# Two wide multiplications of the fp4 rounding move to GpSimd for three late chunks

## The chip, the cores and the metric

The kernel runs on one core of one Trainium2 chip. TensorE multiplies matrices, VectorE (DVE in the profile) and GpSimd (POOL) do elementwise work and reductions, ScalarE (ACT) does activations and copies, and SyncE (SP) issues the DMAs. The metric is the device time of one execution in microseconds (us), as the median of several runs.

## What is computed

The input is x, 8 sequences of 1024 rows of 256 floats. Four stages follow, each as x = x + stage(layernorm(x)): a decoder layer with linear attention and a gelu feed-forward, a relu feed-forward of width 1024, softmax attention over each sequence, and a gated feed-forward whose operands are rounded to fp4. The change touches this last stage:

```python
def fp4_quant_dequant(x):                 # blocks of 16 along the last dimension
    scale = max(abs(xb)) / 6.0            # one per block, at least 1e-12
    q = GRID[searchsorted(MID, abs(xb / scale))] * sign(xb) * scale
gate = fp4_linear(x, w_gate)
y = fp4_linear(x, w_up)                   # 256 -> 704
h = silu(gate) * y
return fp4_linear(h, w_down)              # rounds h (rows of 704) again, 704 -> 256
```

## The kernel before

The rows are cut into 64 chunks of 128 rows, eight to a sequence. The linear attention works on 16 groups of four chunks (`flow` p = 0 to 15), the two dense stages on the same groups, and softmax with the gated stage on single chunks, cc = 0 to 63 (`soft_chunk`, line 1729). All stages run beside each other for different rows. Once the last group has left the linear attention (`linear_attention`, line 1544), its buffers `q` and `k` become two more buffers for gated rows (line 1554); that is why the same operation appears in the profile on `hid`, `q` and `k`, and why `flow`, `x` and `rows` serve beside `prob` and `rows`. Buffer names in the profile are of the tag and not of the stage.

One softmax chunk takes its scores, exponentials, turned probabilities and the product with the values; then a layer norm, the rounding of its 256-wide rows (`fp4(n, D)`, line 1813), the products with the gate and up weights in two halves of 352 columns, tanh on ScalarE and two multiplications on VectorE for each half, and the rounding of the 704-wide gated rows (`fp4(hid, INTER, factor=0.5)`, line 1844). The rounded rows are turned in three pairs of 128 columns (`flip`, line 739), either on TensorE, with a copy by ScalarE, or by a `cut` copy on GpSimd, a transposing DMA to `spun` and a copy by ScalarE. Twelve matmuls with `wdT` (six steps of contraction, each shown as two) give the chunk's output, VectorE adds the rows (`y`), and a DMA stores it.

The rounding (`fp4`, line 802) is, for a width of 704: a reduction to 44 maxima (`x_amax`), the scale `x_s`, its reciprocal `x_r`, a multiplication of the row by `x_r`, a square on ScalarE (`q_c`, kept as bf16), two operations that add and subtract a constant and so round (`hid<-q_c,hid`, twice), and a multiplication by `x_s`. All but the square ran on VectorE.

The order of the instructions is written out by a planner (`Plan`, line 133) while the kernel is built. Each part of the work is a generator that names the queue and the tiles that it needs next; `took` (line 226) estimates what each instruction costs and when its engine and its result are free; `run` (line 380) issues, again and again, the part with the smallest key. The key holds first the wait, then how far the part is from "ripe" (its data must have been there for `ripe_t`, `ripe_v`, `ripe_s`, `ripe_g` or `ripe_d` us, by queue, line 124), then a due time. `idle` (line 365) says whether TensorE has a part ready within `ahead` us; where not, `flip` turns on TensorE. These constants are replaced by others as the planner's clock goes on (`EARLY`, line 78; the last set, line 104, holds from 2150 us of its own clock). `due` (line 470) adds constants that hold for one flow alone (`lin1`, `lin3`). The queue order of each engine is exactly the planner's. Where TensorE would have nothing for 1.6 us, `fill` (line 1883) puts in products of the identity with itself.

Of the kernel before, what the change touches and what calls it, by code (L numbers as in the profile page):

```python
# [14 lines left out]
ALU = mybir.AluOpType  # L15
AX = mybir.AxisListType

P = 128
# [5 lines left out]
INTER = 704  # L24
# [7 lines left out]
    span=-0.073, prods=0.129, pair=0.137, sums=0.037, weighted=0.239, sums2=0.231, chunk=0.625,  # L32
    scores=0.819, turn_k=0.829, xo=0.419, turn_h=0.635, step=0.092, dense=-0.115, norm=0.522,
    soft=3.5, soft1=0.277, soft2=0.575, soft3=0.75, fp4=2.397, fp4_over=4.836, tail=11,
    weights=0.209, shy=0.745, ripe_t=1.247, ripe_v=0.744, ripe_s=0.298, ripe_g=0.0, ripe_d=6.94,
    back=0.511, ahead=0.946, stage=3, lin=0.0, lin0=0.01, lin1=0.0, lin2=0.0, lin3=0.0,
    dense0=0.0, dense1=-0.033, norm0=0.0, norm1=0.0, weights0=-0.412, weights1=0.023, gate0=0,
    gate1=1, gate2=1, by_act=1,
)
LAG = 2  # L40
QB = 16
G = 4
GT = G * P
# [38 lines left out]
        weights=0.082, shy=0.832, ripe_t=0.516, ripe_v=0.135, ripe_s=0.467, ripe_g=0.906,  # L82
        ripe_d=13.418, lin0=-0.645, dense1=-0.003, norm1=-0.276, weights0=-1.017, weights1=0.043,
# [3 lines left out]
        span=-0.064, pair=0.148, sums=-0.114, chunk=0.644, scores=0.581, turn_k=0.911, xo=0.57,  # L87
        dense=0.196, soft=3.213, soft1=0.005, soft2=0.747, fp4_over=6.403, shy=-0.178,
        ripe_t=1.2, ripe_s=0.838, ripe_g=0.043, back=0.505, ahead=0.602, lin=-0.262, lin1=-0.582,
# [6 lines left out]
        weights=0.078, ripe_d=7.107, ahead=0.839, lin2=-0.414, dense1=-0.101, norm1=0.415,  # L96
    )),
    (2150.0, dict(
        span=-0.075, prods=0.106, pair=0.211, sums=0.071, weighted=0.176, chunk=0.596,
# [2 lines left out]
        dense1=0.151, norm0=-0.113, norm1=-0.184, weights0=-0.286, gate1=3, shy=0.438,  # L102
    )),
    (1000000000.0, dict(
        lin3=0.54, ripe_d=5.647, lin1=0.423, dense1=-0.149, scores=0.713, ripe_g=0.203, xo=0.287,
        chunk=0.609, shy=-0.351, back=0.633, sums2=0.302, ripe_t=0.458, soft2=0.808, ahead=1.77,
        step=0.117, span=-0.165, weights=0.128, ripe_s=0.0, fp4=2.485, turn_k=0.743,
    )),
]

# [18 lines left out]
class Plan:  # L129
# [96 lines left out]
    def took(self, queue, op, args, kw):  # L226

        aps = [x for x in list(args) + list(kw.values()) if isinstance(x, bass.AP)]
        outs = [kw["out"] if "out" in kw else aps[0]]
        if kw.get("accum_out") is not None:  # L230
            outs.append(kw["accum_out"])
        size = 1
        for ap in aps:
            n = 1
            for d in ap.shape[1:]:
                n *= d
            size = max(size, n)

        overlap, after = 0.0, 0.035
        if queue == "tensor":  # L240
            size = 1
            for d in outs[0].shape[1:]:
                size *= d
            cost = size * (0.853e-3 if op == "transpose" else 1.687e-3)
            tiled = op == "matmul" and (kw["lhsT"].shape[-1] <= 32 or kw["lhsT"].shape[0] <= 32)
            if tiled or op == "matmul" and kw["lhsT"].dtype == BF16:
                cost *= 0.25
            if tiled != self.tiled:
                cost += 0.2
            self.tiled = tiled  # L250
            after = 0.2
        elif queue == "vector":
            each = {"reciprocal": 6.2e-3, "tensor_tensor_scan": 2.15e-3}.get(op, 1.05e-3)
            cost = 0.17 + each * size
            if op == "tensor_scalar" and outs[0].dtype == BF16:
                cost = 0.16 + 0.26e-3 * size
            elif op == "scalar_tensor_tensor" and any(ap.shape[-1] == 1 for ap in aps):
                cost += 0.06
            if size >= 256 and not any(ap.tensor.name in self.banks for ap in aps):
                cost *= 1.12  # L260
            overlap = 0.08
        elif queue == "scalar":
            cost = (0.16 if op == "copy" and outs[0].dtype != U16 else 0.26) + 0.82e-3 * size
            for x in args:
                if not isinstance(x, bass.AP) and self.SETS.get(x, self.act_set) != self.act_set:
                    self.act_set = self.SETS[x]
                    self.free[queue] = self.free.get(queue, 0.0) + 1.3
            if kw.get("accum_out") is not None:
                cost += 0.15
            overlap = 0.1  # L270
        elif queue == "gpsimd":
            cost = 0.65 + 0.7e-3 * size
            if op in ("tensor_scalar", "iota"):
                cost = 0.22
            elif op == "memset":
                cost = 0.1 + 0.9e-3 * size
            elif op == "tensor_copy":
                cost = 0.2 + 1.0e-3 * size
        else:
            wide = op != "dma_start_transpose" and size > 256  # L280
            cost = 1.34 if op == "dma_start_transpose" else 0.6 if wide else 0.54
        start = self.free.get(queue, 0.0)
        if queue not in ("tensor", "sync"):
            start = max([start] + [self.used.get(ap.tensor.name, 0.0) for ap in outs])
        for ap in aps:
            name = ap.tensor.name
            if self.by.get(name) != queue or queue in ("vector", "gpsimd"):
                start = max(start, self.done.get(name, 0.0) + (0.05 if queue == "gpsimd" else 0.0))
            if name not in self.done and name in self.held:
                start = max(start, self.used[name])  # L290
        if queue == "tensor":
            if start - self.ran > 2.0:
                self.slow = start + 2.1
            if start < self.slow:
                cost *= 2
            self.ran = start + cost
        if queue == "sync":
            start = max(start, self.landed.pop(0))
        end = start + cost
        if queue == "sync":  # L300
            n = 2e-6 / 180e-3 if op == "dma_start_transpose" else 4e-6 / 320e-3
            for d in outs[0].shape:
                n *= d
            self.free["rings"] = max(self.free.get("rings", 0.0), end) + n
            after = self.free["rings"] - end + (0.75 if op == "dma_start_transpose" else 1.8)
            self.landed.append(end + after)
        self.free[queue] = end - overlap
        for ap in outs:
            self.done[ap.tensor.name] = end + after
            self.by[ap.tensor.name] = queue  # L310
        for ap in aps:
            name = ap.tensor.name
            self.used[name] = max(self.used.get(name, 0.0), end + after)
            if queue != "tensor" and name not in self.kept:
                self.held.discard(name)
# [130 lines left out]
def block_stack_kernel(ctx: ExitStack, tc: tile.TileContext, a: dict, out: bass.AP):  # L446
# [20 lines left out]
    plan = Plan(tc, tc.nc)  # L467
# [328 lines left out]
    def blocks(t, width):  # L796
        return t[:, :width].rearrange("p (b e) -> p b e", e=QB)

    def wide(v, rows, nb):
        return v.unsqueeze(2).to_broadcast([rows, nb, QB])  # L800

    def fp4(src, width, rows=P, factor=1.0):

        nb = width // QB
        src = src[:rows, :width]
        amax = small([P, INTER // QB], "x_amax", 2)[:rows, :nb]
        nc.vector.tensor_reduce(
            amax, blocks(src, width), AX.X, ALU.max, apply_absolute_value=True
        )
        sc = small([P, INTER // QB], "x_s", 4)[:rows, :nb]
        nc.vector.tensor_scalar(sc, amax, factor / 6.0, 1e-12, ALU.mult, ALU.max)
        rc = small([P, INTER // QB], "x_r", 3)[:rows, :nb]
        nc.vector.reciprocal(rc, sc)  # L820
        yield dve(rc)
        nc.vector.scalar_tensor_tensor(
            blocks(src, width),
            blocks(src, width),
            -factor * (1.0 - 2.0**-23),
            wide(rc, rows, nb),
            ALU.mult,
            ALU.mult,
        )
        tile_c = yield from fresh("q_c", act(src))  # L830
        c = tile_c[:rows, :width]
        nc.scalar.activation(c, src, AF.Square, scale=(2.0**22 / 6.0) ** 0.5)
        yield dve(c)
        k = 2.0**22 * 4.0 / 3.0
        nc.vector.scalar_tensor_tensor(src, c, k, src, ALU.add, ALU.add)
        yield dve(src)
        nc.vector.scalar_tensor_tensor(src, c, k, src, ALU.add, ALU.subtract)
        plan.drop(tile_c)
        nc.vector.tensor_tensor(
            blocks(src, width), blocks(src, width), wide(sc, rows, nb), ALU.mult  # L840
        )

# [96 lines left out]
    weights = set()  # L939
# [789 lines left out]
    def soft_chunk(cc):  # L1729
# [86 lines left out]
        hid = None  # L1816
# [24 lines left out]
            nc.vector.tensor_tensor(hid[:, cols], hid[:, cols], ub, ALU.mult)  # L1841
        plan.drop(xqT)
        yield dve(hid)
        yield from fp4(hid, INTER, factor=0.5)
        hqT, pairs = [], []
        for half in range(2):
            tq = yield from fresh("prob", plan.pool(hid, at=at + times["soft3"]), "hqT")
# [91 lines left out]
```

## Time and profile before

| what | us |
|---|---|
| median of 3 runs (lowest, highest) | 2448.72 (2447.79, 2450.22) |
| the profiled execution | 2447.88 |
| its span, first to last instruction | 2445.7 |
| TensorE, VectorE, ScalarE, GpSimd busy | 2421.6, 1893.1, 1415.8, 1260.2 |
| 44 maxima of the last five chunks' gated rows taken at | 2399.88, 2411.86, 2413.34, 2417.38, 2428.20 |
| last output added on VectorE at | 2442.57 |

A line of the instructions in order of time has the start, the time taken, engine, line of the kernel (nearly always 427, the planner's helper), operation, output and inputs by their tags, the shape, and how many of the kind stand together; brackets hold the idle time of the engine just before and what ended it. Engines overlap the end of one instruction with the start of the next, so starts can be closer than the durations.

### The profile page before, as it was taken

To read this page: it belongs to the slowest core of one execution; us is meant where nothing else is said; L and a number is where in the kernel's file an instruction comes from. 1 tells how busy PE (TensorE), PEld (TensorE's weight loads), DVE (VectorE), ACT (ScalarE), POOL (GpSimd) and SP (SyncE) were. 2 spreads that over 40 slices of the span, in tenths; PEclk is the share of its full clock that TensorE was granted. 3 is DMA by queue.
4 is the path that set the end of the run, shared out by engine and by line. 5 is a ranking of instruction groups with operands and counts; after the bars stand their busy time and mean duration, and the time that the engine had idled before them with its cause. 6 is when DMAs were issued, how large, how long until landed. Compare 5 with 4: busy or idle time off the path is not lost.

```text
span 2445.7 us, 47558 instructions
## 1 busy us (share of the span) xinstructions
PE 2421.6 (99%) x16449; PEld 1884.0 (77%) x16449; DVE 1893.1 (77%) x4128; ACT 1415.8 (58%) x2936; POOL 1260.2 (52%) x2251
## 2 busy tenths in 40 slices
PE   8999999999999999999999999999999999999999
PEld 6787887877877777777777777778787777877676
DVE  7887777868778787777868778687786878755877
ACT  5546456565555656566565655746657465565563
POOL 4455364555545646366454645545455564544342
PEclk9999999999999999999999999999999999999999
DMA  4454655555555555456464564555565645545341
GB/s 105 108 168 136 177 135 142 126 125 134 126 134 126 138 137 124 131 134 146 119 143 132 130 142 119 133 122 124 142 131 132 139 122 143 126 127 126 65 97 46
DMA packets 627665, 312.34 MB, mean 128 GB/s; under 512 B 430560, under 2 KB 615904, under 8 KB 627424
## 3 DMA queue, kind: packets, MB, share of 16 engines
q1 hardware_dynamic: 627424, 309.31, 52.2%
q8 instruction: 130, 2.13, 0.4%
q14 instruction: 111, 0.91, 0.1%
HBM read 188.43 MB, written 20.97 MB: 86 GB/s over the span
## 4 chain that ended last, share of the span: by engine, by line
PE 83%; DVE 8%; ACT 3%; POOL 2%; issue 2%; DMA 1%; SPq 0%; DVEq 0%; POOLq 0%; ACTq 0%
PE bank L427 83%; DVE prod L427 2%; DVE hid L427 2%; DMA spun<-cut 1%; ACT L427 1%; POOL cut L427 1%; POOL ln_rstd L427 1%; DVE ln_st L427 1%; DVE x_amax L427 0%; DVE u L427 0%; DVE spread L427 0%; POOL ln_shift L427 0%; POOL ln_ve L427 0%; DVE mx L427 0%; DVE res L427 0%
## 5 line engine op out<-in xcount | busy, mean ns | idle before, releaser
L427 PE MATMUL bank<-half,w_in 128*128 128x256 f32 x2048 | 531.0, 382 | 3.1 <-ACT half L427 2.6
L427 PE MATMUL bank<-w_out,hidden 128*128 128x256 f32 x2048 | 526.1, 383 | 1.4 <-ACT hidden L427 1.4
L427 PEld LDWEIGHTS bank<-w_out,hidden 128*128 128x128 f32 x2048 | 376.4, 190 | 100.3 <-issue 44.5
L427 PEld LDWEIGHTS bank<-half,w_in 128*128 128x128 f32 x2048 | 382.8, 190 | 77.1 <-issue 17.2
L427 POOL TENSOR_SCALAR ln_ve<-ln_mv 128x1 f32<-128x1 f32 x384 | 104.5, 272 | 581.7 <-DVE ln_mv L427 554.2
L427 POOL TENSOR_TENSOR ln_rstd<-ln_ve,neghalf 128x1 f32<-128x1 f32 x384 | 236.5, 616 | 31.9
L427 ACT ACTIVATE hidden<-bank,c_L_ffn_b 128x256 f32<-128x256 f32 x256 | 121.1, 473 | 215.4 <-PE bank L427 214.6
L427 PE MATMUL bank<-n2T,qT 128*128 128x512 f32 x512 | 241.8, 595 | 0.2
L427 PE MATMUL bank<-vt,probT 128*128 128x256 f32 x1024 | 231.5, 379 | 0.0
L427 POOL COPY cut<-n 128x512 uint16<-128x512 uint16 x228 | 162.3, 718 | 120.2 <-DVE n L427 85.4
L427 ACT ACTIVATE hidden<-bank,c_L_attn_b 128x256 f32<-128x256 f32 x256 | 120.2, 470 | 175.7 <-PE bank L427 175.0
L427 PEld LDWEIGHTS bank<-vt,probT 128*128 128x128 f32 x1024 | 194.4, 190 | 31.3 <-issue 3.6
L427 POOL COPY cut<-prob 128x512 uint16<-128x512 uint16 x222 | 163.1, 762 | 83.7 <-ACT prob L427 67.0
L427 ACT ACT_TABLE_LOAD x137 | 175.8, 1283 | 12.3 <-PE bank L427 9.1
L427 POOL COPY cut<-hid 128x512 uint16<-128x512 uint16 x165 | 121.5, 755 | 110.0 <-DVE hid L427 66.3
L427 ACT COPY probT<-spun 128x512 uint16<-128x512 uint16 x250 | 162.6, 672 | 25.7 <-DMA spun<-cut 25.3
L427 PE MATMUL bank<-wdT,hqT 128*128 128x256 f32 x768 | 176.6, 380 | 0.8 <-DVE sc L427 0.4
L427 PE MATMUL bank<-wgT,xqT 128*128 128x352 f32 x512 | 173.3, 461 | 0.4 <-DVE sc L427 0.2
L427 PE MATMUL bank<-wuT,xqT 128*128 128x352 f32 x512 | 172.5, 459 | 0.3 <-DVE sc L427 0.3
L427 PEld LDWEIGHTS bank<-wdT,hqT 128*128 128x128 f32 x768 | 145.1, 190 | 23.9 <-issue 1.4
L427 PEld LDWEIGHTS bank<-n2T,qT 128*128 128x128 f32 x512 | 96.1, 190 | 71.2 <-issue 57.6
L427 DVE TENSOR_TENSOR sc<-bank,tri 128x384 f32<-128x384 f32 x240 | 118.1, 545 | 31.8 <-PE bank L427 31.2
(292 smaller groups left out, 4784.4 us busy)
## 6 DMA issues: line engine op xcount, KB each, us to landing
w_in<-in_L_attn_W_dram SPq DMA_DIRECT2D x128, 256.0 KB
w_out<-in_L_attn_W_dram SPq DMA_DIRECT2D x128, 256.0 KB
w_in<-in_L_ffn_w_dram SPq DMA_DIRECT2D x128, 256.0 KB
w_out<-in_L_ffn_w_dram SPq DMA_DIRECT2D x128, 256.0 KB
spread<-packed SPq DMA_DIRECT2D x90, 256.0 KB
spun<-cut SPq DMA_TRANSPOSE x761
x<-in_L_attn_inputs_dram SPq DMA_DIRECT2D x64, 128.0 KB
xr<-in_L_attn_inputs_dram SPq DMA_DIRECT2D x64, 128.0 KB
```

Source lines behind the costliest of these rows:

```text
L427: ins = method(*args, **kw)
```

## The change

For chunks 59, 60 and 61 the multiplication by the reciprocal and that by the scale run on GpSimd (`pooled`). GpSimd's product has no place for the constant factor, so a small multiplication on VectorE puts it into the 44 reciprocals first. The planner's cost of a GpSimd operation wider than 512 is 1.5 us. The last set of due times is replaced.

```diff
+POOLED = (59, 62)
...
-        lin3=0.54, ripe_d=5.647, lin1=0.423, dense1=-0.149, scores=0.713, ripe_g=0.203, xo=0.287,
-        chunk=0.609, shy=-0.351, back=0.633, sums2=0.302, ripe_t=0.458, soft2=0.808, ahead=1.77,
-        step=0.117, span=-0.165, weights=0.128, ripe_s=0.0, fp4=2.485, turn_k=0.743,
+        lin3=0.194, lin1=0.433, dense1=-0.149, scores=0.713, ripe_g=0.582, xo=0.236, chunk=0.609,
+        shy=-0.351, back=0.633, sums2=0.302, ripe_t=0.0, soft2=0.808, ahead=2.087, step=0.117,
+        span=-0.165, weights=0.128, ripe_s=0.0, fp4=2.485, turn_k=0.743,
...
+            elif size > 512:
+                cost = 1.5
...
-    def fp4(src, width, rows=P, factor=1.0):
+    def fp4(src, width, rows=P, factor=1.0, pooled=False):
...
-        nc.vector.scalar_tensor_tensor(
-            blocks(src, width),
-            blocks(src, width),
-            -factor * (1.0 - 2.0**-23),
-            wide(rc, rows, nb),
-            ALU.mult,
-            ALU.mult,
-        )
+        if pooled:
+            nc.vector.tensor_scalar(rc, rc, -factor * (1.0 - 2.0**-23), None, ALU.mult)
+            yield plan.pool(rc)
+            nc.gpsimd.tensor_tensor(
+                blocks(src, width), blocks(src, width), wide(rc, rows, nb), ALU.mult
+            )
+        else:
...
-        nc.vector.tensor_tensor(
+        if pooled:
+            yield plan.pool(src)
+        (nc.gpsimd if pooled else nc.vector).tensor_tensor(
             blocks(src, width), blocks(src, width), wide(sc, rows, nb), ALU.mult
         )
...
-        yield from fp4(hid, INTER, factor=0.5)
+        yield from fp4(hid, INTER, factor=0.5, pooled=POOLED[0] <= cc < POOLED[1])
```

The new set has no `ripe_d` of its own, so that of the base set, 6.94, holds.

More of the change, by code (lines that the diff above doesn't have):

```diff
@@ L821, in fp4 @@
         yield dve(rc)
-        nc.vector.scalar_tensor_tensor(
-            blocks(src, width),
-            blocks(src, width),
-            -factor * (1.0 - 2.0**-23),
-            wide(rc, rows, nb),
-            ALU.mult,
-            ALU.mult,
-        )
+        if pooled:
[5 more added lines that the diff above has]
+        else:
+            nc.vector.scalar_tensor_tensor(
+                blocks(src, width),
+                blocks(src, width),
+                -factor * (1.0 - 2.0**-23),
+                wide(rc, rows, nb),
+                ALU.mult,
+                ALU.mult,
+            )
         tile_c = yield from fresh("q_c", act(src))
```

## The prediction

> **What bounds the kernel now.** I read the page first, then busy time by stretch of the end, then the instructions of TensorE, VectorE and GpSimd in order of time there. Page, first part:
>
> ```profile
> PE 2421.6 (99%) x16449; PEld 1884.0 (77%) x16449; DVE 1893.1 (77%) x4128; ACT 1415.8 (58%) x2936; POOL 1260.2 (52%) x2251
> ```
>
> TensorE has work for 99% of the span, at a granted clock of 0.999; an edit on another engine can only win what TensorE still loses. Where that is, the stretches show (PE, PEld, DVE, ACT, POOL busy; clock; DMA; GB/s):
>
> ```profile
> 2380.00:2400.00 20.00, 20.00 (x82) 15.14 (x81) 17.32 (x37) 10.15 (x20) 6.77 (x13) 1.00 0.25 50
> 2400.00:2420.00 20.00, 20.00 (x80) 14.25 (x79) 19.14 (x39) 8.74 (x17) 2.38 (x3) 1.00 0.20 46
> 2420.00:2436.00 16.00, 13.63 (x93) 11.98 (x91) 15.08 (x22) 5.25 (x10) 4.02 (x4) 1.00 0.18 44
> 2436.00:2446.00 10.00, 6.08 (x28) 4.79 (x28) 1.07 (x3) 2.00 (x5) 0.61 (x1) 1.00 0.24 64
> ```
>
> From 2400 to 2436 VectorE is busy 34.2 of 36 us while GpSimd works 6.4. TensorE looks busy to 2436, but its order of time says with what:
>
> ```profile
> 2418.88 1.35 PE L427 MATMUL bank<-wuT,xqT 128*128 128x352 f32 x4
> 2420.06 4.85 PE L427 MATMUL bank<-ident 128*128 128x128 f32 x42
> 2425.61 0.63 PE L427 MATMUL bank<-ident,hid 128*128 128x128 f32 x4 [0.69 <-DVE hid L427]
> ...
> 2428.91 5.60 PE L427 MATMUL bank<-wdT,hqT 128*128 128x256 f32 x24
> ...
> 2437.88 4.58 PE L427 MATMUL bank<-wdT,hqT 128*128 128x256 f32 x20 [0.35 <-ACT hqT L427]
> ```
>
> The last gate-and-up product ends at 2420.2; then come 42 filler products (ident on ident) and holes that VectorE ends. Of the 22.4 us from 2420.06 to 2442.46, real work is 0.63 + 0.66 + 5.60 + 0.38 + 0.63 + 1.03 + 4.58 = 13.5 us. So 8.9 us are lost there, 9.7 with 0.83 us of filler at 2414.43. The chain of waits agrees: between 2399 and 2436 nearly every piece is a VectorE instruction of `hid`, `q` or `k` (the buffers of the gated rows).
>
> Which chunk is which follows from the reductions of a 704-wide row (2399.88, 2411.86, 2413.34, 2417.38, 2428.20: the last five, so chunks 59 to 63). The change takes 59, 60 and 61. Their multiplications by 1/scale start at 2401.92, 2415.77 and 2416.57, by scale at 2409.01, 2424.57 and 2426.30: all where VectorE is full.
>
> **What the change takes from VectorE.** Neighbouring wide operations follow each other every 0.80 us (2415.77, 2416.57, 2417.38); the one at 2426.30 takes 1.1. Six go: 5 x 0.80 + 1.1 = 5.1 us. Three small multiplications on 128x44 come in, priced by the x_s row (186 ns median, 0.2 us in sequence): 0.6 us. Net **4.5 us**.
>
> **What GpSimd pays.** No 128x704 product runs on GpSimd in the trace. Nearest rows: its 128x256 product takes 728 ns, its 128x1 TENSOR_SCALAR 190 ns. A start of 0.19 and (728 - 190)/256 = 2.1 ns a column gives 1.67 us; scaling 728 by 704/256 gives 2.0 us; the lower bound is VectorE's own 0.89. I take 1.67. Six are 10 us beside 6.4 us of work in 36. No layer norm is left in GpSimd's queue after 2398.4, so only the `cut` copies of these chunks stand behind the products.
>
> **The shared access.** What speaks against the change stands in these lines:
>
> ```profile
> 602.07 0.89 DVE L427 TENSOR_TENSOR hid<-hid,x_s 128x704 f32<-128x704 f32 x1
> 602.13 1.42 POOL L427 TENSOR_TENSOR res<-res,b_L_ffn_b 128x256 f32<-128x256 f32 x1
> ```
> ```profile
> 1411.59 2.37 DVE L427 SCALAR_TENSOR_TENSOR hid<-q_c,hid 128x704 f32<-128x704 bf16 x2 [0.52 <-ACT q_c L427]
> 1411.84 1.37 POOL L427 TENSOR_TENSOR res<-n,b_L_attn_bo 128x256 f32<-128x256 f32 x1
> ```
>
> The 0.73 us product on GpSimd that begins inside a VectorE operation with two SBUF inputs ends 0.59 us after it: it ran behind it. The VectorE pair at 1411.59 takes 2.37 where two alone take 1.69: the second waited 0.68 us. So the two exclude each other, and while GpSimd holds its turn VectorE may only do operations that do not need it. Of this kind seem x_amax (at 602.88 it runs through) and those reading a PSUM bank. A 1.67 us product holds VectorE's next two-input operation up to about 1.5 us. The Trainium skill says this too (Advanced Engine Details and Errata, GPSIMD Details): Pool shares a read and a write interface with VectorE and conflicts with operations of two SBUF inputs; the trace agrees, by 0.68 us here. The skill would leave such a product on VectorE (GPSIMD Engine Reference, Engine selection), at about twice the time; at 1.67 to 0.89 the rows agree, and by the page, as an estimate, the six would take six times 1.78, some 10.7 us.
>
> Now place by place, in the order of before. First product of 59 (ready 2401.5): VectorE follows with bank operations, then one n step: 0.2 us of wait. Second of 59 (2409): bank operations and a reduction follow until 2415: none. First of 60 (2413.6) and of 61 (behind it, 2415.3 to 2417): reductions, reciprocals and bank operations follow: none. ScalarE's square, q_c, can start at 2415.4 and 2417.1 instead of 2416.75 and 2417.55, so the longer product is covered, and the tanh queued behind it on ScalarE is not late. The second products of 60 and 61 (before: 2424.57, 2426.30) fall between the two-input steps of 61 and 62. One can lie beside the last chunk's bank operations and reduction (1.0 + 1.4 us), the other not: 0 to 3.0 us of wait, I take 0.8. Together 1.0: **3.5 us** stay.
>
> **What is late next.** The last chunk's final multiplication ends at 2435.88; 6.6 us later TensorE ends, and 3.2 us of y and its transfer follow. TensorE's 20 products at 2437.88 waited for chunk 62's turned block by DMA (ScalarE's copy at 2437.15). That chunk moves up with VectorE; 0 to 1.6 us of the 6.6 may go, since a turn by cut, DMA and copy has some 3.9 us of its own (2409.96 to 2413.87). I take 0.5. Four groups of 12 products are 10.6 us, so TensorE need not bind earlier.
>
> **The due times.** `lin1` and `lin3` apply to flows 1 and 3 alone, done long before 2150; `xo` to linear chunks, over when q and k become buffers (GpSimd's MEMSET at 2151.34). What acts: ripe_t 0.458 to 0, ripe_g 0.203 to 0.582, ripe_d 5.647 to 6.94, ahead 1.77 to 2.087. They re-sort the last 290 us. TensorE has no hole from 2150 to 2420 but 0.2 us in the stretches, so a new order has nothing to win there; it can lose, or close holes behind 2420. Bounds: -5 to +7 us; I take 0.
>
> **Sum.** 4.5 - 1.0 + 0.5 = 4.0 us off the profiled execution's 2447.88 (span 2445.7 and 2.2 around it): 2443.9. The median shown, 2448.72, lies 0.84 higher, so I forecast **2444.7**.
>
> **The rivals**, by the median.
> *The gain is eaten* (0.18): both late products wait fully (3.0), or the cuts behind them delay TensorE's groups for 60 and 61; 4.5 - 3.2 to -1: 2447.2 to 2450.2. For it: the two-input steps stand close at 2420 to 2427. Against: reductions and bank steps stand between.
> *The new order also closes holes* (0.14): limit 9.2 us, the last chunk's chain alone from 2420.3 (steps 0.5, 0.9, 0.6, 0.8, 0.9, 0.8, 0.9, 0.9: 2426.7 instead of 2435.88). Gains of 6.5 to 9: 2439.7 to 2442.2. For it: eight fillers twice and 42 once. Against: five chunks share VectorE.
> *Slower by the shared access* (0.10): each of the six products makes VectorE wait in full. 6 x 1.5 = 9.0 against 4.5 saved: +4.5; at 2.0 us a product 6 x 1.85 = 11.1: +6.6; 2453.2 to 2455.3. It decides from a mean wait of 0.75 us a product. Against: the rows after the first products of all three chunks.
> *Slower by the new order* (0.08): one or two turns of 3.9 us come late for TensorE between 2150 and 2420: 2452.6 to 2456.5.
> That the products don't move can't be: the branch depends on the chunk's number alone.
>
> **How the numbers follow.** The forecast, a gain of 2 to 6.5 (2442.2 to 2446.7), gets 0.50. What a measurement can tell from no change is 0.2%, 4.9 us: 2443.8 to 2453.6. Of the forecast a third lies below (0.18), with the second rival's 0.14: faster 0.32. Of the slower ones 0.14 lies above. Same: 0.54. The range, 2440.0 to 2451.5, leaves out both slower rivals and a corner of the second, about 0.2.
>
> **What would show it.** Six 128x704 products on GpSimd at 1.6 to 2.0 us, longer where they begin in a two-input step; VectorE some 4.5 us less busy; the last chunk's final multiplication near 2432; less filler after 2420. Wrong, if that multiplication isn't earlier, if VectorE's wide steps stretch beyond 2 us, or if TensorE shows holes before 2414.

## The result, and the profile after

The changed kernel takes **2444.69 us** in the median (2441.99 to 2447.81, 22 runs) beside 2448.73 for the kernel before (2446.55 to 2450.22, 22 runs): a ratio of **0.9984 [0.9978, 0.9991]**, 4.0 us less. The forecast was 2444.7. A second set of runs of the same kernel, further down, gave 2444.65 and 0.9984 [0.9975, 0.9993]. The profiled execution took 2445.43 us, its span 2443.7.

The page of after, first part; then busy time by stretch (PE, PEld, DVE, ACT, POOL; clock; DMA; GB/s):

```profile
PE 2416.6 (99%) x16393; PEld 1879.1 (77%) x16393; DVE 1888.3 (77%) x4125; ACT 1412.2 (58%) x2936; POOL 1265.2 (52%) x2253
```
```profile
2400.00:2420.00 20.00, 17.64 (x63) 11.84 (x63) 18.86 (x36) 9.39 (x19) 11.95 (x13) 0.95 0.28 66
2420.00:2436.00 16.00, 13.58 (x58) 10.36 (x58) 11.39 (x18) 4.34 (x9) 3.27 (x3) 0.93 0.22 34
2436.00:2446.00 10.00, 4.29 (x17) 3.37 (x15) 0.42 (x1) 1.12 (x3) 0.00 (x0) 0.85 0.08 28
```

VectorE is 4.8 us less busy over the span, and from 2400 to 2436 it works 30.3 us instead of 34.2 while GpSimd works 15.2 instead of 6.4. What was not expected stands in TensorE's columns: from 2400 to 2420 it is busy 17.6 of 20 us, where it was 20.0 before, and the granted clock falls to 0.95, 0.93 and 0.85. TensorE's instructions there:

```profile
2417.28 2.10 PE L430 MATMUL bank<-wgT,xqT 128*128 128x352 f32 x4 [2.13 <-ACT xqT L430]
2419.17 2.43 PE L430 MATMUL bank<-wuT,xqT 128*128 128x352 f32 x4
...
2427.51 5.49 PE L430 MATMUL bank<-wdT,hqT 128*128 128x256 f32 x24
2435.34 1.54 PE L430 MATMUL bank<-ident,hid 128*128 128x128 f32 x6 [2.34 <-DVE hid L430]
2436.67 3.62 PE L430 MATMUL bank<-wdT,hqT 128*128 128x256 f32 x12
```

TensorE issues 56 products less; the 58 fillers behind 2420 are gone. Behind the last chunk's final multiplication only that chunk's own six turning products and twelve `wdT` products are left, where before chunk 62's twelve stood there too (the 20 at 2437.88). The hole of 2.13 us waits for ScalarE's copy of the last chunk's turned rows, and the two groups of four products behind it take 2.10 and 2.43 instead of 1.35.

GpSimd's instructions show the six products, 59's at 2397.91 and 2404.72, 60's at 2406.33 and 2411.43, 61's at 2415.47 and 2420.80:

```profile
2397.91 1.39 POOL L430 TENSOR_TENSOR hid<-hid,x_r 128x704 f32<-128x704 f32 x1 [5.13 <-DVE x_r L430]
...
2404.72 1.50 POOL L430 TENSOR_TENSOR hid<-hid,x_s 128x704 f32<-128x704 f32 x1 [2.74 <-DVE hid L430]
2406.33 1.50 POOL L430 TENSOR_TENSOR hid<-hid,x_r 128x704 f32<-128x704 f32 x1
...
2411.43 1.39 POOL L430 TENSOR_TENSOR hid<-hid,x_s 128x704 f32<-128x704 f32 x1 [0.89 <-DVE hid L430]
2412.88 1.72 POOL L430 COPY cut<-hid 128x512 uint16<-128x512 uint16 x3
2415.47 1.38 POOL L430 TENSOR_TENSOR q<-q,x_r 128x704 f32<-128x704 f32 x1 [0.87 <-DVE x_r L430]
2420.80 2.11 POOL L430 TENSOR_TENSOR q<-q,x_s 128x704 f32<-128x704 f32 x1 [3.94 <-DVE q L430]
```

Each takes 1.38 to 1.50 us but the last, which begins 0.02 us after the VectorE step below and takes 2.11. The order differs from that of before: 60's second product and its three cuts are done before 61's first product starts. VectorE beside them:

```profile
2405.22 1.03 DVE L430 TENSOR_SCALAR x_r<-x_r 128x44 f32<-128x44 f32 x1
...
2408.78 2.50 DVE L430 SCALAR_TENSOR_TENSOR hid<-q_c,hid 128x704 f32<-128x704 bf16 x2
...
2420.78 0.89 DVE L430 SCALAR_TENSOR_TENSOR k<-q_c,k 128x704 f32<-128x704 bf16 x1
```

The small multiplication at 2405.22 takes 0.85 more than the 0.18 of its like: it ends with the product at 2404.72 to 2406.22. It is the one large wait of VectorE behind a product. The pair at 2408.78 lies beside GpSimd's cuts and takes 2.50, where a pair that nothing disturbs takes 1.82 (at 2432.54).

**How single profiles are compared here.** GpSimd's MEMSET of `q`, where linear attention is over, falls between 2149.90 and 2154.41 us in the profiles of this study, though the work before it is the same in all of them. That spread of 4.5 us is as large as what is to be explained. So in the table the times of the end run from that MEMSET: to the start of the last chunk's 44 maxima (M), to the end of its final multiplication (E), and to the start of the last `y`. "Change again" is the second set of runs of the changed kernel. Each ratio is to the runs of before that were taken beside that kernel (medians 2448.73 to 2448.84); the kernels of the experiments have 11 runs each.

| kernel | median (range, runs), us | ratio to before | M | E | E to `y` | last `y` |
|---|---|---|---|---|---|---|
| before | 2448.73 (2446.55–2450.22, 22) | 1 | 276.86 | 284.54 | 6.69 | 291.23 |
| changed | 2444.69 (2441.99–2447.81, 22) | 0.9984 [0.9978, 0.9991] | 277.57 | 285.38 | 5.05 | 290.43 |
| change again | 2444.65 (2443.54–2447.7, 11) | 0.9984 [0.9975, 0.9993] | 276.33 | 283.68 | 3.85 | 287.53 |
| products on GpSimd, old due times | 2447.32 (2445.33–2448.89) | 0.9993 [0.9984, 1.0001] | 273.95 | 282.88 | 7.01 | 289.89 |
| new due times, products on VectorE | 2447.70 (2447.26–2452.7) | 0.9997 [0.9988, 1.0006] | 278.72 | 285.17 | 6.42 | 291.59 |
| order of after, products on VectorE | 2447.92 (2446.45–2451.61) | 0.9996 [0.9988, 1.0005] | 280.27 | 287.05 | 3.85 | 290.90 |
| order of before, products on GpSimd | 2449.75 (2448.44–2451.75) | 1.0005 [0.9996, 1.0014] | 276.04 | 286.21 | 6.46 | 292.67 |
| the same, 60 and 61 only | 2449.42 (2446.49–2454.14) | 1.0004 [0.9995, 1.0013] | 274.90 | 285.07 | 6.47 | 291.54 |
| the same, a cut put ahead | 2448.66 (2447.38–2455.11) | 1.0002 [0.9993, 1.0011] | 275.06 | 285.90 | 6.47 | 292.37 |
| changed, holes filled | 2444.76 (2442.61–2448.72) | 0.9983 [0.9974, 0.9992] | 276.25 | 282.83 | 4.54 | 287.37 |
| changed, two copies exchanged | 2445.17 (2443.62–2449.29) | 0.9985 [0.9976, 0.9994] | 276.25 | 283.76 | 3.86 | 287.62 |
| exchanged, ten fillers | 2446.38 (2442.81–2447.48) | 0.9988 [0.9979, 0.9997] | 276.36 | 283.75 | 5.29 | 289.04 |
| exchanged, 8 and 5 fillers | 2444.86 (2442.51–2448.97) | 0.9986 [0.9977, 0.9994] | 276.15 | 282.93 | 3.86 | 286.79 |

The last column is one execution each. Taken against before, it agrees with the medians to within 1.4 us, but for the first profile of the changed kernel, whose end is 2.9 us longer than in the second profile. In the second the hole is the same and the clock is not (1.00 from 2415 to 2425, where the first has 0.79 and 0.87):

```profile
2418.71 1.45 PE L430 MATMUL bank<-wgT,xqT 128*128 128x352 f32 x4 [2.13 <-ACT xqT L430]
2419.99 1.35 PE L430 MATMUL bank<-wuT,xqT 128*128 128x352 f32 x4
```

In the first profile VectorE waits 1.51 us at 2424.23 for the output of TensorE's slow products, which makes M 1.2 later. The second profile is taken for the changed kernel in what follows, because it agrees with the medians: 287.53 beside 291.23, 3.7 us less, as the medians have 4.0.

### The profile page after: what moved, and what is told of

It reads as the page before. It is cut to its first block, busy times and chain, and to the rows that moved or that the text cites. A ratio compares the mean times of both kernels' runs of the same rounds, so it can differ in the third digit from the quotient of the medians.

```text
span 2443.7 us, 47413 instructions
## 1 busy us (share of the span) xinstructions
PE 2416.6 (99%) x16393; PEld 1879.1 (77%) x16393; DVE 1888.3 (77%) x4125; ACT 1412.2 (58%) x2936; POOL 1265.2 (52%) x2253
## 3 DMA queue, kind: packets, MB, share of 16 engines
q8 instruction: 130, 2.13, 0.4%
## 4 chain that ended last, share of the span: by engine, by line
PE 88%; DVE 6%; ACT 3%; POOL 1%; DMA 1%; issue 1%; SPq 0%; DVEq 0%; POOLq 0%; ACTq 0%
PE bank L430 88%; DVE prod L430 2%; DVE hid L430 1%; ACT L430 1%; DMA spun<-cut 1%; DVE ln_st L430 0%; DVE u L430 0%; POOL ln_rstd L430 0%; DVE spread L430 0%; POOL cut L430 0%; POOL ln_shift L430 0%; DVE res L430 0%; DVE sc L430 0%; DVE div L430 0%; DMA w_in<-in_L_attn_W_dram 0%
## 5 line engine op out<-in xcount | busy, mean ns | idle before, releaser
L430 PEld LDWEIGHTS bank<-half,w_in 128*128 128x128 f32 x2048 | 382.9, 190 | 76.8 <-issue 17.6
L430 PEld LDWEIGHTS bank<-vt,probT 128*128 128x128 f32 x1024 | 194.2, 190 | 30.3 <-issue 2.4
```

The costliest lines, as they stand in the source:

```text
L430: ins = method(*args, **kw)
```

## The experiments

Of the theories, the first two ask whether the move or the new due times bring the gain; the later ones ask what the move costs in GpSimd's queue, and whether the holes on TensorE cost anything. Single kernels have intervals of about 0.09% to either side, 2.2 us, so most verdicts need the traces too. All kernels compute the whole reference.

### Each half alone, the order planned anew

Old due times with the products on GpSimd is the changed kernel with the last `EARLY` set of before; new due times alone is

```diff
-POOLED = (59, 62)
+POOLED = (64, 64)
```

> The six products on GpSimd, with the due times of before; the planner sorts the work again. Theory 1 (the gain is VectorE's relief, the due times add nothing): 4 us below the kernel before, near 2444.7, that is like the changed kernel. Theory 2 (the gain is the new order, and the move as such only pays for shared access): within 1 us of before, 2447.7 to 2449.7, or above it.

> The new due times with all products on VectorE. Theory 1: within 1.5 us of before, 2447.2 to 2450.2, since TensorE has no holes from 2150 to 2400 that an order could close. Theory 2: 3 to 4 us below before. A third reading, that the new due times fit only together with the move: above before by 3 us or more, with VectorE as full at the end as before and the last chunk later.

Measured: 1.4 us less than before with the move alone, 1.0 less with the due times alone; neither interval excludes no change, and together they would make 2.4 and not 4.0. The first lies between the two theories' figures; the second is within the 1.5 us of the first theory, and its trace is 0.4 longer than before's. In both the planner wrote another order than in either kernel, so neither is a part of the change in the strict sense. This called for kernels in which the order of every queue is held.

### Each half alone, the order held

A helper issues an instruction on one queue, while the planner counts it on another. So every other instruction stays where it was in the order, and the products stand in their queue at the same point.

```diff
+def elsewhere(queue, counted, op, as_op, *args):
+    ins = getattr(getattr(tc.nc, queue), op)(*args)
...
+    plan.last[queue] = ins.ins.name
+    plan.took(counted, as_op, args, {})
...
-nc.gpsimd.tensor_tensor(blocks(src, width), ...)
+elsewhere("vector", "gpsimd", "tensor_tensor", "tensor_tensor", blocks(src, width), ...)
```

That is the order of after with the six products on VectorE; it keeps the three small multiplications. The order of before with the products on GpSimd has the reverse, and the small multiplication by the constant ahead of the first product. In the traces every other instruction of TensorE, VectorE, ScalarE and GpSimd stands in the order of the kernel that it is compared with.

> Every engine's order is that of before, but the six products are issued on GpSimd at the same points, with the small multiplication ahead of the first one on VectorE; no part is sorted anew. Theory 1: the last chunk's final multiplication on VectorE ends 3 to 4 us earlier and the time falls by 2.5 to 4 us. Rival (shared access eats the gain in an order not made for it): the wide two-input steps on VectorE stretch by over 3 us in sum and the time is within 1 us of before.

> Every engine's order is that of the changed kernel, but the six products run on VectorE at the same points of the order. Theory 1: the end moves back by some 4 us against the changed kernel, to 2448 to 2450. Theory 2 (the order alone): it stays within 1 us of the changed kernel, 2443.7 to 2445.7.

Measured: in the order of before the move brings nothing (2449.75, 1.0 us more than before, interval 0.9996 to 1.0014). The order of after alone brings 0.8 by the median (interval 0.9988 to 1.0005) and 0.3 by the trace. Within the order of after the move takes 2447.92 to 2444.69, 3.2 us (medians of resampled runs differ by 2.3 to 4.8 in 95 of 100), and 290.90 to 287.53 by the trace, 3.4. **The gain is the move's, but only in the new order.**

VectorE in the order of after with the products on it, the first products of 59 and 60, the last chunk's maxima and its final steps:

```profile
2399.17 1.34 DVE L806 TENSOR_TENSOR hid<-hid,x_r 128x704 f32<-128x704 f32 x1
...
2408.74 1.29 DVE L806 TENSOR_TENSOR hid<-hid,x_r 128x704 f32<-128x704 f32 x1
...
2431.47 0.89 DVE L430 TENSOR_REDUCE x_amax<-hid 128x44 f32<-128x704 f32 x1
...
2435.51 1.82 DVE L430 SCALAR_TENSOR_TENSOR hid<-q_c,hid 128x704 f32<-128x704 bf16 x2 [0.79 <-ACT q_c L430]
2437.36 0.89 DVE L430 TENSOR_TENSOR hid<-hid,x_s 128x704 f32<-128x704 f32 x1
```

And the same work in the second profile of the changed kernel:

```profile
2427.59 0.89 DVE L430 TENSOR_REDUCE x_amax<-hid 128x44 f32<-128x704 f32 x1
...
2432.20 1.82 DVE L430 SCALAR_TENSOR_TENSOR hid<-q_c,hid 128x704 f32<-128x704 bf16 x2 [1.43 <-ACT q_c L430]
2434.05 0.89 DVE L430 TENSOR_TENSOR hid<-hid,x_s 128x704 f32<-128x704 f32 x1
```

With the MEMSET at 2151.20 and 2151.26 the times can nearly be subtracted as they stand. The maxima come 3.9 us earlier by the move. Then VectorE waits for ScalarE's square, 1.43 instead of 0.79, and 0.6 of it is lost again. Behind the final multiplication both take 3.85 to the last `y`, and before took 6.69: those 2.8 us are the order's, which does chunk 62's output products earlier and turns all three pairs of the last chunk on TensorE. The same order, with the small multiplications (0.3), costs 3.4 us at M and 2.5 at E, so alone it is worth next to nothing.

Where the gain goes in the order of before can be followed from GpSimd's queue there, with one step of VectorE:

```profile
2409.71 1.39 POOL L804 TENSOR_TENSOR hid<-hid,x_s 128x704 f32<-128x704 f32 x1 [5.19 <-DVE hid L428]
2411.05 0.60 POOL L428 COPY cut<-n 128x512 uint16<-128x512 uint16 x1
...
2425.62 1.90 POOL L804 TENSOR_TENSOR hid<-hid,x_s 128x704 f32<-128x704 f32 x1 [7.01 <-DVE hid L428]
2427.48 2.03 POOL L804 TENSOR_TENSOR q<-q,x_s 128x704 f32<-128x704 f32 x1
2429.46 0.60 POOL L428 COPY cut<-hid 128x512 uint16<-128x512 uint16 x1
```
```profile
2426.39 1.88 DVE L428 SCALAR_TENSOR_TENSOR k<-q_c,k 128x704 f32<-128x704 bf16 x1
```

Chunk 60's rows are done at 2427.52, and their cut stands behind 61's product until 2429.46. The last chunk's own cut of `n` stands behind 59's product. The rival of this run, wide steps on VectorE stretched by over 3 us in sum, is not what is seen: one wide step waits behind a product, by 1.00 (1.88 instead of 0.88), and two steps on 44 values by 0.40 and 0.27, 1.7 in all. TensorE's waits (us in total, times, longest) from 2395 on:

```profile
PE bank L428 <- ACT xqT L428: 1.7, 1, 1.7
PE bank L428 <- POOL q L804: 1.3, 1, 1.3
PE bank L428 <- ACT hqT L428: 1.3, 1, 1.3
```

and VectorE, for the output of chunk 60, whose `y` stands in its queue ahead of the last chunk's rounding steps:

```profile
2435.29 0.42 DVE L428 TENSOR_TENSOR y<-bank,x 128x256 f32<-128x256 f32 x1 [2.46 <-PE bank L428]
```

In the table: M comes 0.8 us earlier than before, E 1.7 later.

### Which of the products costs it

Two kernels in the order of before: one leaves 59 on VectorE, the other also holds 61's second product back until chunk 60's cut is issued.

```diff
-POOLED = (59, 62)
+POOLED = (60, 62)
...
+        if lets and waiting:      # chunk 60, behind its cut
+            elsewhere("gpsimd", None, "tensor_tensor", "", *waiting.pop())
```

> As the kernel with the order of before and the products on GpSimd, but chunk 59 stays on VectorE, so that no product stands ahead of the last chunk's cut of n in GpSimd's queue. Theory 3 (in the order of before the move frees VectorE, but the product by scale of chunk 59 holds back that cut, and TensorE waits 1.7 us for it): TensorE's wait for xqT goes, the last gate-and-up product is back near 2420 to 2421, and the time falls to 1 to 2.5 us below before, 2446.2 to 2447.7. Rival (shared access eats it): no wait for xqT, but still within 0.5 us of before or above it.

> The order of before with products of chunks 60 and 61 on GpSimd, and one exchange in GpSimd's queue against the run before_order_60_61: chunk 60's cut comes ahead of chunk 61's second product. Theory 6 (in the old order the gain is lost because GpSimd works off its queue in order: chunk 60's cut stands behind chunk 61's product of 2.0 us, so its turned block, TensorE's output group, VectorE's y and, behind y, the last chunk's rounding all come late): TensorE's wait of 1.3 us for the turned block goes, the last chunk's final multiplication comes 1 to 2 us earlier, the time falls 1 to 2.5 us below that run, to 2447 to 2448.5. Rival (VectorE's waits for shared access cost the gain): within 0.5 us of that run.

Leaving 59 out took away the wait for `xqT`, as expected, and M came 1.1 us earlier; but the median hardly moved (2449.42 after 2449.75). VectorE still waited 2.46 for `y`, TensorE 1.28 for `hqT`. With the cut first, the wait for `hqT` is gone and the products run on, yet TensorE now waits longer for 61's rows. Its longest wait and VectorE's `y` there:

```profile
PE bank L428 <- POOL q L743: 1.9, 1, 1.9
```
```profile
2433.81 0.42 DVE L428 TENSOR_TENSOR y<-bank,x 128x256 f32<-128x256 f32 x1 [2.74 <-PE bank L428]
```

The median is 0.8 lower (2448.66), a little less than what was expected and within the intervals; from the MEMSET the trace is 0.8 longer. In that profile TensorE's granted clock is 0.83 from 2425 to 2435, behind the hole of 1.90 us, where the kernel without the exchange has 1.00; the next fillers and output products there are

```profile
2428.67 1.91 PE L428 MATMUL bank<-ident 128*128 128x128 f32 x8
2430.37 5.99 PE L428 MATMUL bank<-wdT,hqT 128*128 128x256 f32 x24
```

instead of the 1.06 and 5.60 us of before. So the exchange may have won what slow products took back; the medians can't tell, and that the place of that one cut costs time is not shown.

What all three kernels share is the 2.5 to 2.7 us that VectorE waits for `y` of chunk 60 between M and E, which before does not have (M to E is 7.7 us there, and 10.2 to 10.8 in the three). The ends of the second products, counted from the MEMSET, say more: chunk 60's rows are ready at 274.12 in before and at 275.37, 274.23 and 274.39 in the three. A product takes longer on GpSimd, and what VectorE saves is used up by it; so chunk 60's `y`, which stands in VectorE's queue ahead of the last chunk's rounding, cannot come earlier, though M does by 0.8 to 2.0. Behind that the three differ: in the kernel without 59, 60's cut starts at 276.17 instead of 274.24, which is the queue; with the cut ahead it starts at 274.45, but 61's rows are ready at 276.95 instead of 276.14, and the slow products follow. In the second profile of the changed kernel chunk 60's rows are ready at 262.99, and VectorE adds its `y` at 2424.07 without a wait. This is read from the traces; no kernel here tried it by itself, and how much of the loss is the longer product and how much the queue stays open.

### Do TensorE's holes cost anything?

The change's TensorE has holes of 2.13 us ahead of the last chunk's gate products and 2.0 to 2.3 ahead of its turn. Two ways were tried: ten filler products in each, and another order of ScalarE's copies that makes the first hole smaller (the last chunk's `xqT` is copied ahead of chunk 60's `hqT`, which waits for its DMA), with and without fillers at the end.

```diff
+            if cc == B * NCH - 1 and j0 == 0:
+                warm(10)
...
-        flips_h = flip_all(pairs, at + times["soft3"])
+        flips_h = flip_all(pairs, at + times["soft3"], warmed=cc == B * NCH - 1)
```
```diff
+        if swapped:               # chunk 60: counted here, issued behind the last chunk's xqT
+            plan.took("scalar", "copy", turned_back, {})
+            later_copy.append(turned_back)
...
+        if cc == B * NCH - 1:
+            elsewhere("scalar", "copy", *later_copy.pop())
```

> The changed kernel with ten filler products on TensorE ahead of each of its two long holes (before the last chunk's first gate product, before its gated rows are turned); all other instructions and orders are the same. Theory 4 (the changed kernel lost the filler that kept TensorE's clock up, and pays for it with slow products behind each hole and with its wide spread): granted clock 1.0 to the end, products behind the holes at 1.35 and 2.75 us instead of 2.10, 2.43 and 3.62, a median 1 to 2.5 us below the changed kernel and a spread of some 2 us instead of 6. Rival (the holes themselves cost, not the clock): within 0.5 us of the changed kernel.

> The changed kernel with one pair of neighbouring ScalarE copies exchanged: the last chunk's turned n (xqT) comes ahead of chunk 60's turned block, whose DMA lands later. Theory 5 (TensorE's hole of 2.1 us at 2415 is a wait in ScalarE's queue behind a DMA that GpSimd's longer product made late): the hole closes, the last gate-and-up product ends 2 to 4 us earlier, the time falls by 1.5 to 3.5 us. Rival (the end is set by VectorE's load and the turned block of chunk 62, so a hole before it costs nothing): within 0.7 us of the changed kernel.

> That exchange and the ten fillers ahead of the last hole alone. Theories 4 and 5 together: 3 to 5 us below the changed kernel, near 2440.5, with a small spread. If only the clock counts, as the changed kernel with fillers; if only the queue, as the one with the exchange.

The holes closed. TensorE with the fillers (line 783), then with the exchange:

```profile
2418.07 2.40 PE L783 MATMUL bank<-ident 128*128 128x128 f32 x20
2420.38 1.45 PE L430 MATMUL bank<-wgT,xqT 128*128 128x352 f32 x4
2421.67 1.35 PE L430 MATMUL bank<-wuT,xqT 128*128 128x352 f32 x4
```
```profile
2417.83 1.35 PE L430 MATMUL bank<-wgT,xqT 128*128 128x352 f32 x4
...
2427.98 0.88 PE L430 MATMUL bank<-ident,k 128*128 128x128 f32 x6 [1.72 <-DVE k L430]
2428.88 7.13 PE L430 MATMUL bank<-wdT,hqT 128*128 128x256 f32 x24
```

With fillers the gate products take 1.45 and 1.35, as they did without them in the second profile of the changed kernel. With the exchange they start 2.4 us earlier than in the second profile, counted from the MEMSET (265.06 and 267.45), but a new hole of 1.72 opens ahead of chunk 62's turn, and the 24 products behind it take 7.13 instead of 5.5. Neither moves the median: 2444.76 and 2445.17, with ten fillers at the end 2446.38, beside 2444.69. In the last kernel the same hole of 1.72 is there, the 24 products take 7.00, and the fillers behind them begin at 2435.24, 0.7 before the last rows are ready, and hold the turn back to 2437.47: its way from E to `y` is 5.29 instead of 3.86. So one more pair was run: the exchange with eight fillers ahead of chunk 62's turn and five ahead of the last, and the changed kernel once more.

> The changed kernel with the exchange of two ScalarE copies, and fillers only where that version has its holes: eight ahead of chunk 62's turn, five ahead of the last chunk's. If the exchange's gain was lost to slow products behind the hole of 1.7 us (7.13 us for 24 products instead of 5.45): 1 to 2 us below the changed kernel, 2442.7 to 2443.7. If the end hangs on VectorE's and GpSimd's chain for chunks 61 and 62 whatever TensorE does: within 0.7 us of the changed kernel.

> The changed kernel once more, beside the others on the same chip and with a second profile. If its end varies from execution to execution with the clock behind its holes, the stretch from the clearing of q (GpSimd's MEMSET near 2150) to the last y differs from the 290.4 us of the first profile by over 1 us; if the spread comes from the first 2150 us, that stretch is 290 to 291 again. The median should be 2444 to 2445.5.

The 24 products are back at 5.45 us, and the end is the shortest of all in the trace (286.79), but the median, 2444.86, is that of the changed kernel, 2444.65. So the expected gains of 1 to 5 us did not come, nor the narrow spread (2442.61 to 2448.72 with fillers): in the median neither the holes nor the copies' order cost anything that these runs can tell, though a gain of 1 us would not be seen. In a single execution a hole can cost: the two profiles of the changed kernel differ by 2.9 us from the MEMSET to the last `y`, by slow products behind their holes. But for that first profile M lies between 276.15 and 276.36 in all of these kernels, wherever TensorE's holes are, which speaks for VectorE's chain through chunks 61 to 63; no version here beats the changed kernel.

## Why the prediction was right, and where it was not

The time was right (2444.7 forecast, 2444.69 measured). Step by step, by the second profile of the changed kernel and the kernel with its order and the products on VectorE:

- **VectorE gets rid of 5.1 us.** The six products take 1.27, 0.80, 1.21, 0.80, 0.81 and 0.80 from start to the next start, 5.7 us; 0.9 of it because two of them run against GpSimd's cuts (1.34 and 1.29 instead of 0.89). Mis-sized by 0.6.
- **Three small multiplications, 0.6.** They take 0.1 each in sequence where they don't wait: 0.3. Both kernels compared here have them; in the one with the products on VectorE each first product starts 0.2 behind its small multiplication, 0.35 more in all.
- **Waits for the shared access, 1.0.** Beside the products right in size, wrong in place: 0.85 at the small multiplication at 2405.22 and 0.14 at a rounding step of `n` (0.56 instead of 0.42), where 59's second and 60's first product run; none at the second products of 60 and 61, where 0.8 was put. In the order of before, where the forecast placed them, they are 1.7, of it 1.27 at those second products.
- **A term that the sum lacks: GpSimd's cuts hold VectorE up as well.** Beside cuts four steps of the changed kernel take 0.72, 2.51, 0.42 and 1.18 us where the other kernel has 0.42, 2.10, 0.19 and 0.89; one step of the other, 0.82 for 0.41, goes the other way: 0.8 lost. Longer waits for ScalarE take 0.3 (0.51 for 59's square beside a wait of 0.25). So 5.7 + 0.35 - 1.0 - 0.8 - 0.3 makes the 3.9 that are seen at M; at E it is 3.4, where 3.5 was forecast.
- **GpSimd's 1.67 for a product.** 1.38 to 1.50 undisturbed, 2.11 once, begun inside a VectorE step as the rows at 602 had it. Near enough; in the changed kernel nothing hung on it.
- **"Only the `cut` copies of these chunks stand behind the products."** Wrong: the last chunk's cut of `n` does too, and the cuts lead through a DMA, a copy and a group of products to a `y` in VectorE's own queue. In the order of before the end waits for that `y` and the whole gain is gone; this is the first rival ("the gain is eaten", 2447.2 to 2450.2), and the kernel with the order of before, at 2449.75, is its case. (The rival's own terms, 4.5 - 3.2 and -1, give 2447.4 to 2449.7, not the bounds written beside them.) The forecast worked place by place in the order of before, where the move gains nothing, so this step failed there and the forecast was saved by the new order.
- **0.5 off behind the last chunk.** 2.8 us went there, all by the order.
- **The due times, 0.** Right as a sum (0.3 to 0.8), but as the difference of two large terms: +2.5 at E and -2.8 behind it. And with the move they are worth more than alone: without them the move gives 2447.32, with them 2444.69.
- **The final multiplication near 2432.** Wrong: 2434.94 and 2435.28 in the two profiles, only 0.9 earlier than before from the MEMSET at best, since the order costs 2.5 there.
- **"Wrong, if TensorE shows holes before 2414."** A hole of 2.13 us came, at 2415. It was no sign of a lost gain: closing it changed nothing that could be measured.

The sum was 4.0 and the traces have 3.7, but from other terms: 3.5 + 0.5 + 0 in the forecast, 3.4 + 0 + 0.3 for the move at E, the move behind it, and the order. That it met the median to 0.01 us is luck at a spread of over 5 us between runs.

## What to carry to other kernels

An operation moved to another in-order queue has to be judged with the queue order that it meets: the same six products were worth 3.2 us in an order that has chunk 60's rows ready well before the end waits for them, and nothing in one where its `y` is what the last chunk waits behind. Before trusting a move, follow what stands behind it in the new queue through to the engine that was relieved, for the chain may come back to it. Where a kernel's long first part varies by more than the effect, measure the end from a marker in each trace, hold every queue's order while one thing is changed, and take two profiles.

## What the runs showed of the hardware

- **The clock behind a hole differs from run to run.** Behind the hole of 2.13 us the four gate and the four up products took 2.10 and 2.43 us in one execution of the changed kernel (granted clock 0.79 from 2415 to 2420, 0.87 to 2425) and 1.45 and 1.35 in another (1.00); behind one of 4.20 us, in its order with the products on VectorE, 2.46 and 2.07 (0.66 from 2420 to 2425). The Trainium skill (TensorE: Matmul & The Clock Gate, "What's actually happening") has a free-running window of some 3.4 us of idleness that lowers the clock. The hole of 4.20 agrees, and so does the change from run to run, but the first profile shows that a hole well under that window can be followed by slow products.
- **GpSimd holds up more of VectorE than operations with two inputs.** The 128x44 multiplication by a constant took 1.03 instead of 0.18 us beside a product, the scale step on 44 values 1.02 instead of 0.19 (at 2426.95 in the kernel with the cut ahead), and GpSimd's 16-bit cuts lengthened VectorE's products from 0.89 to 1.34 and 1.29.
- **A product of 128x704 takes GpSimd 1.38 us and VectorE 0.89**, 1.6 times as long, where the 128x256 product (0.73 us) had let 1.67 be expected.
- **The first 2150 us of the same work took 2149.90 to 2154.41 us** in thirteen profiles. What makes this spread was not looked into. Over whole runs part of the spread goes with TensorE's clock: the five runs of the changed kernel at a granted clock of 0.998 took 2446.05 to 2447.29 us, the six at 1.0 took 2443.04 to 2444.85.
